# A decoder layer on one core: the rows of a block turned one block later, next to the turn-in, and three smaller moves

## The chip, the core and the metric

The kernel runs on one core of a Trainium2 chip. The metric is the device time of one execution in microseconds; "before" is the median of three runs. All data are fp32. The engines are TensorE (PE), VectorE (DVE), ScalarE (ACT), GpSimd (POOL) and SyncE (SP), which here issues nearly all DMA.

## What is computed

There are 16 x 256 = 4096 tokens of 256 channels, and three sublayers, each followed by a layer norm. Cut to what matters:

```python
# 1: squared-relu attention against fixed keys and values, 4 heads of 64 channels
q = layernorm(x, ln_g, ln_b).reshape(B, T, 4, 64)      # k = w_fc rows, v = w_proj.T rows: 1024 x 64
out = square(relu(einsum(q, k))) @ v
x = layernorm(x + (x + out))                            # so 2 x + out is normalized
# 2: cross attention, 16 heads of 16 channels, to ctx (16 batches of 256 rows)
attn = gamma * (Q K^T) / 4 + delta * (alpha_pos * max(D, 0) + alpha_neg * min(D, 0))   # D = clip(frac_k - frac_q, +-0.2)
x = layernorm(x + softmax(attn) V Wo^T + bo)
# 3: feed-forward of 1024 with the low-rank term of one expert of eight, chosen by argmax of the gate
x = layernorm(x + relu(x Wi^T + b + lora[top1](x)) Wo^T + b2)
```

## The kernel before

Everything is written in an order of its own (`tc.manual_schedule()`, L941): each engine runs its instructions in the order in which the program emits them, and waits come from the data and from tile pools, whose buffers are reused in turn. A pool's tile with `bufs=2` makes the third request wait until all readers of the first are done. So the order of emission is the order of each queue, SP's and GpSimd's too.

**Stage one** (L965 to L1044) is the first sublayer, in eight blocks of 512 rows (class Block, L249). A block is kept as `x` (four tiles of 128 rows), and is normalized, turned (128x128 transposes on TensorE) into `xnT` (channels on partitions, two halves `c`), and then goes through 16 pairs (c, n): `scores` (L327), four 64x64 matmuls into a tile of two PSUM banks (pool psA, two such tiles, four banks), a relu on ScalarE (L340), a square on VectorE (L342); and `values` (L345), four 64x64 matmuls that add into two banks of psV. The loop over m (L1022) takes eight steps a block: two scores, the values of the step before (`behind`), and then the pieces that the lists `steps[m]` hold. After the last values of a half c, `keep` (L360) copies the sums to `oT`, with two ScalarE copies and a GpSimd addition (L367); for c = 0 that is in step 4, for c = 1 in step 0 of the next block. In the steps of block tb lie, beside that:

- step 0: the last two rows of `norm_out` for block tb - 2 (L987)
- step 1: `turn_out` of block tb - 1 (L369): eight transposes of `oT` in two one-bank tiles of psB, each read by a VectorE instruction that makes y = 2 x + out (L383); then `measure_out(0)`, row statistics on VectorE (L185, L186); step 2: `measure_out(1)`
- steps 3 and 4: `measure` of the next block, and in step 3 the load of x of the block after that
- step 5: `scale` (L962): Ln and Exp on ScalarE (L194, L196) and four small VectorE instructions (L202 to L240), for eight rows of statistics: four of the next block's input, four of the last block's output
- step 6: `norm_in` of the next block, four ScalarE rows (L245)
- step 7: between the scores and the values, `turn_in` of the next block, eight transposes (L313), one half read by ScalarE (L317) and one by VectorE (L322); after the values two rows of `norm_out` of block tb - 1: a ScalarE instruction (L245) and a GpSimd addition of `bo` (L407) for each tile of 128 rows

Blocks 2 to 6 also make the clipped differences of `frac` that stage two needs (`clip`, L538: one VectorE instruction, L528, and for some batches a DMA to DRAM) in steps 0 and 7 (`slots`, L955). Block 1 also computes `biases` (L139), block 7 also the first batch's turn, keys and queries for stage two (`early`, L958; L1018 to L1021), with the queries in step 6, read by ScalarE (L481).

**Stage two** (L1059 to L1203) runs 64 groups (16 batches of four groups; a group is four heads of 256 x 256 logits) with the logits, maxima, exponentials and `attend` of neighbouring groups interleaved. psA's four banks become the four banks of logits. The feed-forward of a block of 512 rows (second class Block, L748) is spread over eight groups, part 0 to 7, from n = 15 on. In part 1, `gates` (L800) multiplies by the gate and the low-rank weights (128x64 matmuls) and copies the result on ScalarE (L813); it stands after the large piece of that group, `queries` (L461), and before `turned(2)`, `turned(3)` (L675, transposes) and their exponentials (L690). The large piece has two halves, TensorE's and the read of its bank (L476 on VectorE in these groups). `late` (L1154) says whether the second half is emitted at once or only after those exponentials. Banks for transposes and these products come from `tile_b` (L50): psB's two, and every third request psV's "W".

Of the kernel before, what the change touches and what calls it, by code (L numbers as in the profile page):

```python
# [14 lines left out]
P = 128  # L15
# [7 lines left out]
def tile_decoder_layer(ctx: ExitStack, tc: tile.TileContext, a: dict, out: bass.AP):  # L23
# [208 lines left out]
    if True:  # L232
# [16 lines left out]
        class Block:  # L249
# [119 lines left out]
            def turn_out(self, jj):  # L369
# [4 lines left out]
                ps = tile_b()  # L374
# [15 lines left out]
                )  # L390

# [353 lines left out]
    if True:  # L745
        out_view = out.rearrange("(b j p) c -> b p j c", j=4, p=P)

        class Block:  # L748
# [51 lines left out]
            def gates(self):  # L800

                ps = tile_b()
                for c in range(CC):
                    for t in range(2):
                        nc.tensor.matmul(
                            ps[64 * t : 64 * t + 64, 0:256],
                            lhsT=gw[:, c, :],
                            rhs=self.xT[:, c, 256 * t : 256 * t + 256],
                            start=(c == 0),
                            stop=(c == CC - 1),  # L810
                        )
                self.gT = small.tile([P, 256], FP, tag="spread", bufs=1, name="gT")
                nc.scalar.copy(self.gT, ps[:, 0:256])  # L813
# [127 lines left out]
    with tc.manual_schedule():  # L941
# [13 lines left out]
        slots = [(tb, m) for tb in range(2, 7) for m in (0, 7)]  # L955
        assert len(slots) == len(clips)
        first = batches[0]
        early = [first.turned(), first.keys(), first.queries(), first.vals()]  # L958
# [6 lines left out]
        for tb in range(NB):  # L965
# [4 lines left out]
            if tb == 0:  # L970
                nc.vector.memset(mv, 0.0)
            if 0 < tb < NB - 1:
                last = rows_in[tb - 1]
                for jj in range(2):
                    steps[1].append(lambda jj=jj: [*last.turn_out(jj)])
                steps[1].append(lambda: last.measure_out(0))
                steps[2].append(lambda: last.measure_out(1))
                last.mv = mv[:, 4:8]
                for j in range(2, 4):
                    steps[7].append(  # L980
                        lambda j=j, tb=tb: last.norm_out(by[tb], 4 + j, j, nc.gpsimd)
                    )
            if tb > 1:
                older = rows_in[tb - 2]
                for j in range(2):
                    steps[0].append(
                        lambda j=j, tb=tb: older.norm_out(by[tb - 1], 4 + j, j, nc.gpsimd)  # L987
                    )
            if tb + 1 < NB:
                nxt = rows_in[tb + 1]  # L990
                steps[3].append(lambda: nxt.measure(0))
                steps[4].append(lambda: nxt.measure(1))
                steps[5].append(lambda tb=tb, mv=mv: scale(tb, mv))
                steps[6].append(lambda tb=tb: nxt.norm_in(by[tb]))
                nxt.mv = mv[:, 0:4]
                turning = [lambda: nxt.turn_in(0), lambda: nxt.turn_in(1)]
            else:
                turning = []
            if tb + 2 < NB:
                steps[3].append(rows_in[tb + 2].load)  # L1000
# [17 lines left out]
            if tb + 1 == NB:  # L1018
                steps[4] += [lambda: groups[0].negative(3)]
                for m, together in ((4, early[:2]), (6, early[2:3])):  # L1020
                    steps[m] += [lambda p=piece: step(p) for piece in together * 2]  # L1021
            for m in range(8):  # L1022
# [4 lines left out]
                if m == 7:  # L1027
                    for piece in turning:
                        piece()
# [5 lines left out]
                for piece in steps[m]:  # L1035
                    piece()
        for block, *args in behind:
# [21 lines left out]
        for n in range(N + 2):  # L1059
# [22 lines left out]
            if n == N:  # L1082
                six.gates()
            if n > N:
                six.inner(0, range(0, 1))
            if older and not halved and not apart and n != N:
                if 0 <= n - 1 - FIRST < 8 * FUSED and (n - 1 - FIRST) % 8 in (5, 7):
                    groups[n - 3].attend()
                older.attend()
            if nxt:  # L1090
# [36 lines left out]
            else:  # L1127
                if nxt:
                    nxt.positive(0)
                    nxt.positive(1)  # L1130
                if last:
# [22 lines left out]
            late = (n % 4 == 0 or n == 1) and not ff  # L1154
# [9 lines left out]
            if ff and part == 1 and n < N:  # L1164
                ff.gates()
# [63 lines left out]
        seven.gates()  # L1229
        seven.inner(0, range(0, 1))  # L1230
# [85 lines left out]
```

## Time and profile before

| what | value |
|---|---|
| median of three runs | 903.74 us (903.57 to 930.24) |
| the profiled execution | 903.41 us, span 901.6 us, clock 0.999 |
| stage one, first scores to last values | 9.4 to 255.1 us |
| stage two with the fused feed-forward | 255.1 to about 824 us |
| last feed-forward blocks | to 901.6 us |
| PE busy in 9.44 to 255.10 | 245.08 of 245.66 us |
| PE busy in 345 to 824 | 478.05 of 479.00 us |
| DVE, ACT, POOL busy in 9.44 to 255.10 | 207.14, 178.52, 55.62 us |
| L342 squares, 128x1024 | 128 of them, mean 1255 ns |
| L340 relus, 128x1024 | 128 of them, mean 1022 ns |

How to read the profile lines: in a timeline, the columns are start (us), time from the first start to the last end (us), engine, line of the kernel, operation, output <- inputs, tile sizes and count; neighbouring instructions of one line are merged into one row, and in brackets stands how long the engine sat idle before it and for what. An fp32 matmul shows as two records. In the list of waits, the columns are total us, number, and longest us.

### The profile page before, as it was taken

How to read it: one execution, taken by the hardware profiler on the slowest of the kernel's cores; microseconds unless marked ns; L12 is line 12 of the kernel's file. 1: busy time of each engine (PE TensorE's matmuls, PEld its weight loads, DVE VectorE, ACT ScalarE, POOL GpSimd, SP SyncE). 2: the span in 40 equal slices, each digit the busy share in tenths (PEclk: the TensorE clock that was granted, in tenths of full speed). 3: DMA queues.
4: the chain of work that ended last, by engine and by line, in shares of the span. 5: the costliest groups of instructions: out<-in, count | busy, mean ns of one | idle time of the engine just before them, and what ended most of it. 6: DMA issues, size and time to landing. Idle time of an engine off the chain costs nothing.

```text
span 901.6 us, 19050 instructions
## 1 busy us (share of the span) xinstructions
PE 888.9 (99%) x6940; PEld 546.7 (61%) x6940; DVE 710.4 (79%) x1976; ACT 569.2 (63%) x947; POOL 394.7 (44%) x385
## 2 busy tenths in 40 slices
PE   8999999999999999999999999999999999999997
PEld 4333333333366777577668757766875786586555
DVE  6888899889669999778777887877788787778444
ACT  5767787778687888366565846656684675566111
POOL 1102312231569998435633654563465357344010
PEclk9999999999999999999999999999999999999999
DMA  5411011100001222010111102011110201111101
GB/s 139 147 36 36 31 39 39 65 2 1 13 1 54 70 70 57 13 42 21 36 48 39 48 14 66 20 36 46 41 49 13 67 18 38 42 28 44 23 1 47
DMA packets 44190, 37.01 MB, mean 41 GB/s; under 512 B 14912, under 2 KB 40000, under 8 KB 44096
## 3 DMA queue, kind: packets, MB, share of 16 engines
q1 hardware_dynamic: 43520, 35.52, 14.5%
q8 instruction: 55, 0.90, 0.4%
q14 instruction: 39, 0.32, 0.1%
q10 hardware_dynamic: 576, 0.26, 0.1%
HBM read 21.07 MB, written 6.03 MB: 30 GB/s over the span
## 4 chain that ended last, share of the span: by engine, by line
PE 83%; DVE 10%; ACT 4%; issue 2%; DMA 1%; SPq 1%; DVEq 0%; ACTq 0%
PE ps_l L876 12%; PE ps_b L683 11%; PE ps_v L352 10%; PE ps_a L332 10%; PE ps_b L906 7%; PE ps_l L643 6%; PE ps_v L699 6%; PE ps_v L906 4%; PE ps_b L595 3%; PE ps_b L465 3%; DVE pr L342 3%; PE ps_b L491 2%; PE ps_b L513 2%; DVE neg L658 2%; PE ps_l L888 2%
## 5 line engine op out<-in xcount | busy, mean ns | idle before, releaser
L622 POOL TENSOR_SCALAR neg<-dneg,aneg,delta 128x512 f32<-128x512 f32 x217 | 189.0, 882 | 183.5 <-PE ps_b L683 125.3
L658 DVE CUSTOM_DVE_ANT_0 neg<-ps_l,neg 128x256 f32<-128x256 f32 x512 | 181.4, 420 | 26.5 <-PE ps_l L643 23.6
L634 ACT ACTIVATE ps_l<-dpos,apos_d 128x512 f32<-128x512 f32 x256 | 173.2, 687 | 41.4 <-DVE mx L658 36.8
L342 DVE TENSOR_TENSOR pr<-r 128x1024 f32<-128x1024 f32 x128 | 155.4, 1255 | 33.5 <-ACT r L340 33.3
L690 ACT ACTIVATE pT<-ps_b 128x512 f32<-128x512 f32 x256 | 142.6, 590 | 56.3 <-PE ps_b L683 54.3
L340 ACT ACTIVATE r<-ps_a 128x1024 f32<-128x1024 f32 x128 | 126.4, 1022 | 57.3 <-PE ps_a L332 32.8
L683 PE MATMUL ps_b<-ident,neg 128*128 128x128 f32 x1024 | 138.8, 277 | 2.1 <-ACT pT L690 2.0
L683 PEld LDWEIGHTS ps_b<-ident,neg 128*128 128x128 f32 x1024 | 113.2, 141 | 37.4 <-issue 16.1
L673 POOL TENSOR_TENSOR neg<-neg,mx 128x1024 f32<-128x1024 f32 x65 | 124.2, 1912 | 22.8 <-DVE mx L658 21.7
L352 PE MATMUL ps_v<-pr,vv 64*64 64x512 f32 x1024 | 123.4, 593 | 0.3
L332 PE MATMUL ps_a<-xnT,kT 64*64 64x512 f32 x1024 | 122.1, 592 | 0.5 <-ACT r L340 0.3
L876 PE MATMUL ps_l<-xt,wi 128*128 128x512 f32 x248 | 111.5, 595 | 0.0
L673 DVE TENSOR_TENSOR neg<-neg,mx 128x1024 f32<-128x1024 f32 x63 | 95.7, 1519 | 0.3
L367 POOL TENSOR_TENSOR xt<-xt,half 128x512 f32<-128x512 f32 x15 | 23.8, 1584 | 136.9 <-ACT half L366 136.9
L352 PEld LDWEIGHTS ps_v<-pr,vv 64*64 64x64 f32 x1024 | 38.1, 132 | 70.6 <-issue 44.3
L332 PEld LDWEIGHTS ps_a<-xnT,kT 64*64 64x64 f32 x1024 | 37.8, 133 | 67.6 <-issue 54.8
L876 PEld LDWEIGHTS ps_l<-xt,wi 128*128 128x128 f32 x248 | 45.3, 190 | 49.0 <-issue 44.4
L643 PE MATMUL ps_l<-kM,qT 32*128 32x256 f32 x1024 | 74.1, 400 | 0.0
L407 POOL TENSOR_TENSOR hid<-hid,bo 128x256 f32<-128x256 f32 x32 | 29.4, 935 | 89.6 <-ACT hid L245 70.8
L906 PE MATMUL ps_b<-wof,hT 128*128 128x256 f32 x304 | 68.4, 380 | 0.0
L699 PE MATMUL ps_v<-pT,vaug 128*32 128x256 f32 x1024 | 66.4, 384 | 0.0
L899 DVE TENSOR_SCALAR hT<-ps_l,wib 128x512 f32<-128x512 f32 x43 | 29.8, 745 | 43.8 <-PE ps_l L888 43.8
(129 smaller groups left out, 1082.6 us busy)
## 6 DMA issues: line engine op xcount, KB each, us to landing
cT<-in_ctxT SPq DMA_DIRECT2D x16, 256.0 KB
kM<-keys SPq DMA_DIRECT2D x128, 32.0 KB
v<-raw SPq DMA_DIRECT2D x128, 32.0 KB
invs<-rows SPq DMA_DIRECT2D x128, 32.0 KB
x<-in_x SPq DMA_DIRECT2D x7, 512.0 KB
out<-x SPq DMA_DIRECT2D x7, 512.0 KB
frow<-in_frac SPq DMA_DIRECT2D x16, 128.0 KB
wi<-in_wiT SPq DMA_DIRECT2D x1, 1024.0 KB
```

The costliest lines, as they stand in the source:

```text
L332: nc.tensor.matmul(sc[64 * k : 64 * k + 64, h, :], lhsT=kT[64 * h : 64 * h + 64, q, hf * P + 64 * k : hf * P + 64 * k + 64], rhs=self.xnT[ ...
L342: nc.vector.tensor_tensor(pr, r, r, ALU.mult)
L352: nc.tensor.matmul(self.acc[k][64 * h : 64 * h + 64, :], lhsT=vv[64 * k : 64 * k + 64, hf, 64 * q : 64 * q + 64], rhs=pr[64 * k : 64 * k + ...
L622: nc.gpsimd.tensor_scalar(self.neg[:, g], self.batch.dneg, aneg[:, h : h + 1], delta, ALU.mult, ALU.mult,)
L634: nc.scalar.activation(banks[g], self.batch.dpos.rearrange("p j k -> p (j k)"), AF.Copy, scale=apos_d[:, h : h + 1],)
L643: nc.tensor.matmul(banks[g][:, j * S : (j + 1) * S], lhsT=self.batch.qT[rows, self.o, j * P : (j + 1) * P], rhs=self.batch.kM[rows, self.i ...
L658: nc.vector.tensor_tensor_reduce(out=self.t[:, g, j, :], in0=banks[g][:, j * S : (j + 1) * S], in1=self.neg[:, g, j, :], scale=1.0, scalar ...
L673: eng.tensor_tensor(rows, rows, top.to_broadcast([P, 4, S]), ALU.subtract)
L683: nc.tensor.transpose(ps[:, k * S + j * P : k * S + (j + 1) * P], self.t[:, g, j, k * P : (k + 1) * P], ident,)
L690: nc.scalar.activation(self.pT[:, g, :], self.ps[g], AF.Exp)
L876: nc.tensor.matmul(self.banks[g], lhsT=wi[:, c, f * P : (f + 1) * P], rhs=self.xT[:, c, :], start=(c == 0), stop=False,)
L906: nc.tensor.matmul(ps[:, 0:C], lhsT=self.hT[f][:, j * P : (j + 1) * P], rhs=wof[:, f, :], start=(f == 0), stop=(f == FC - 1),)
```

## The change

- Rows out: `turn_out` of block tb - 1 moves from step 1 of block tb to after its last step, as `turn_rows`, eight transposes into one two-bank tile of psA (the pool of the scores) in place of two tiles of psB. Its two L383 instructions follow there.
- `turn_in` of the next block moves from step 7's middle to right behind `turn_rows`, so that nothing stands between it and the next block's scores.
- `measure_out` of block tb - 2 is in steps 1 and 2, its four rows of `norm_out` in step 6 (three) and step 7 (one); `scale` is in step 4, after `measure(1)`; `norm_in` in step 5; the clips in steps 5 and 6; the load of x of block tb + 1 in step 0 of block tb.
- The first batch's queries move from step 6 to step 7 of block 7, and VectorE reads them.
- Stage two: `gates` stands after `attend`, before `turned(0)`, with its copy (`keep_gates`) after `positive(1)`; the second half of `queries` in these groups is late.

```diff
@@ -366,12 +366,13 @@
                 nc.scalar.copy(half, self.acc[1])
                 nc.gpsimd.tensor_tensor(self.oT[:, c, :], self.oT[:, c, :], half, ALU.add)

-            def turn_out(self, jj):
+            def turn_out(self, jj, ps=None):
                 if self.tb >= NB - 2:
                     self.y = hid[:, 4 * self.tb : 4 * self.tb + 4, :]
                 elif jj == 0:
                     self.y = px.tile([P, 4, C], FP, tag="y", bufs=1, name="y")
-                ps = tile_b()
+                if ps is None:
+                    ps = tile_b()
                 for j in range(2):
                     for c in range(CC):
                         nc.tensor.transpose(
@@ -388,6 +389,12 @@
                     ALU.mult,
                     ALU.add,
                 )
+
+            def turn_rows(self):
+
+                ps = psA.tile([P, 2, 512], FP, tag="A", name="ps_a")
+                for jj in range(2):
+                    [*self.turn_out(jj, ps[:, jj, :])]

             def turn_both(self):
                 first, second = self.turn_out(0), self.turn_out(1)
@@ -799,7 +806,7 @@

             def gates(self):

-                ps = tile_b()
+                ps = self.gps = tile_b()
                 for c in range(CC):
                     for t in range(2):
                         nc.tensor.matmul(
@@ -809,8 +816,10 @@
                             start=(c == 0),
                             stop=(c == CC - 1),
                         )
+
+            def keep_gates(self):
                 self.gT = small.tile([P, 256], FP, tag="spread", bufs=1, name="gT")
-                nc.scalar.copy(self.gT, ps[:, 0:256])
+                nc.scalar.copy(self.gT, self.gps[:, 0:256])

             def route(self):
                 ps = tile_b()
@@ -952,10 +961,10 @@
         clips = [
             (batches[b], which) for b in [*range(2, MADE), 0, 1] for which in ("dneg", "dpos")
         ]
-        slots = [(tb, m) for tb in range(2, 7) for m in (0, 7)]
+        slots = [(tb, m) for tb in range(2, 7) for m in (5, 6)]
         assert len(slots) == len(clips)
         first = batches[0]
-        early = [first.turned(), first.keys(), first.queries(), first.vals()]
+        early = [first.turned(), first.keys(), first.queries(True), first.vals()]
         behind = []
         by = [None] * (NB + 1)

@@ -967,37 +976,32 @@
             steps = [[] for _ in range(8)]

             mv = small.tile([P, 8, 2], FP, tag="mv8", bufs=2, name="mv8")
-            if tb == 0:
+            if tb in (0, 1, NB - 1):
                 nc.vector.memset(mv, 0.0)
-            if 0 < tb < NB - 1:
-                last = rows_in[tb - 1]
+
+            if tb > 1:
+                last = rows_in[tb - 2]
+                last.mv = mv[:, 4:8]
                 for jj in range(2):
-                    steps[1].append(lambda jj=jj: [*last.turn_out(jj)])
-                steps[1].append(lambda: last.measure_out(0))
-                steps[2].append(lambda: last.measure_out(1))
-                last.mv = mv[:, 4:8]
-                for j in range(2, 4):
-                    steps[7].append(
+                    steps[1 + jj].append(lambda jj=jj: last.measure_out(jj))
+                for j in range(4):
+                    steps[6 + j // 3].append(
                         lambda j=j, tb=tb: last.norm_out(by[tb], 4 + j, j, nc.gpsimd)
                     )
-            if tb > 1:
-                older = rows_in[tb - 2]
-                for j in range(2):
-                    steps[0].append(
-                        lambda j=j, tb=tb: older.norm_out(by[tb - 1], 4 + j, j, nc.gpsimd)
-                    )
+            turning = []
             if tb + 1 < NB:
                 nxt = rows_in[tb + 1]
-                steps[3].append(lambda: nxt.measure(0))
-                steps[4].append(lambda: nxt.measure(1))
-                steps[5].append(lambda tb=tb, mv=mv: scale(tb, mv))
-                steps[6].append(lambda tb=tb: nxt.norm_in(by[tb]))
                 nxt.mv = mv[:, 0:4]
-                turning = [lambda: nxt.turn_in(0), lambda: nxt.turn_in(1)]
-            else:
-                turning = []
-            if tb + 2 < NB:
-                steps[3].append(rows_in[tb + 2].load)
+                if tb:
+                    steps[0].append(nxt.load)
+                for jj in range(2):
+                    steps[3 + jj].append(lambda jj=jj: nxt.measure(jj))
+                steps[5].append(lambda tb=tb: nxt.norm_in(by[tb]))
+                if tb:
+                    turning.append(rows_in[tb - 1].turn_rows)
+                turning += [lambda: nxt.turn_in(0), lambda: nxt.turn_in(1)]
+            if tb + 1 < NB or tb > 1:
+                steps[4].append(lambda tb=tb, mv=mv: scale(tb, mv))
             if tb == 0:
                 steps[0] += [load_cross]
                 steps[2] += [load_ffn]
@@ -1017,16 +1021,13 @@
                 steps[5].append(batches[1].load)
             if tb + 1 == NB:
                 steps[4] += [lambda: groups[0].negative(3)]
-                for m, together in ((4, early[:2]), (6, early[2:3])):
+                for m, together in ((4, early[:2]), (7, early[2:3])):
                     steps[m] += [lambda p=piece: step(p) for piece in together * 2]
             for m in range(8):
                 c, n2 = divmod(m, 4)
                 coming = []
                 for n in (2 * n2, 2 * n2 + 1):
                     coming.append((now, c, n, now.scores(c, n)))
-                if m == 7:
-                    for piece in turning:
-                        piece()
                 for block, c, n, pr in behind:
                     block.values(c, n, pr)
                     if n == 7:
@@ -1034,6 +1035,8 @@
                 behind = coming
                 for piece in steps[m]:
                     piece()
+            for piece in turning:
+                piece()
         for block, *args in behind:
             block.values(*args)
         scored.close()
@@ -1081,12 +1084,15 @@
                 now.logits()
             if n == N:
                 six.gates()
+                six.keep_gates()
             if n > N:
                 six.inner(0, range(0, 1))
             if older and not halved and not apart and n != N:
                 if 0 <= n - 1 - FIRST < 8 * FUSED and (n - 1 - FIRST) % 8 in (5, 7):
                     groups[n - 3].attend()
                 older.attend()
+            if ff and part == 1 and n < N:
+                ff.gates()
             if nxt:
                 nxt.negative(4 if 1 <= n < FIRST - 1 or (ff and part < 2) else 3)
             if prep:
@@ -1128,6 +1134,8 @@
                 if nxt:
                     nxt.positive(0)
                     nxt.positive(1)
+                if ff and part == 1 and n < N:
+                    ff.keep_gates()
                 if last:
                     last.turned(0)
                     last.exps(0)
@@ -1151,7 +1159,7 @@
             if inverse:
                 inverse.invert()
             step(large_piece)
-            late = (n % 4 == 0 or n == 1) and not ff
+            late = n == 1 or n % 4 == 0 and (not ff or part == 1)
             if not late:
                 step(large_piece)

@@ -1161,8 +1169,6 @@
                 ff.turn(nc.scalar.copy)
                 if nxt:
                     nxt.positive(3)
-            if ff and part == 1 and n < N:
-                ff.gates()
             divided = batches[b - 2] if og == 0 and b >= 2 else None
             if divided and ff:
                 divided.divide()
@@ -1227,6 +1233,7 @@
         seven.biased()
         six.finish(2)
         seven.gates()
+        seven.keep_gates()
         seven.inner(0, range(0, 1))
         seven.route()
         seven.inner(0, range(1, 3))
```

## The prediction, made before the changed kernel was run

> **What bounds the kernel.** I read the page's busy shares and its chain first, then the timeline of TensorE through stage one, then ScalarE, VectorE and GpSimd over one block of it.
>
> ```profile
> PE 888.9 (99%) x6940; PEld 546.7 (61%) x6940; DVE 710.4 (79%) x1976; ACT 569.2 (63%) x947; POOL 394.7 (44%) x385
> ...
> PEclk9999999999999999999999999999999999999999
> ...
> PE 83%; DVE 10%; ACT 4%; issue 2%; DMA 1%; SPq 1%; DVEq 0%; ACTq 0%
> ```
>
> TensorE is the bound at full clock, so time comes or goes only where its stream gets shorter or gets a hole. "99%" doesn't show holes, because a matmul that waits can be drawn longer; the start-to-start distance does. TensorE, block 5 (its steps 3, 4 and 7, the turn, and the first scores of block 6):
>
> ```profile
> 173.52 2.22 PE L352 MATMUL ps_v<-pr,vv 64*64 64x512 f32 x16
> 175.57 1.90 PE L332 MATMUL ps_a<-xnT,kT 64*64 64x512 f32 x16
> ...
> 185.87 1.90 PE L332 MATMUL ps_a<-xnT,kT 64*64 64x512 f32 x16
> 187.69 1.09 PE L313 MATMUL ps_b<-ident,xn 128*128 128x128 f32 x8
> 188.72 1.95 PE L352 MATMUL ps_v<-pr,vv 64*64 64x512 f32 x16
> 190.48 1.90 PE L332 MATMUL ps_a<-xnT,kT 64*64 64x512 f32 x16
> ```
>
> Undisturbed, eight score or value matmuls (16 records) take 1.72 us to the next start, so a step of both takes 3.43 and eight steps 27.47. A turn of eight transposes costs 1.18: 185.87 to 190.48 is 4.61 against 3.43. Step 3 has a hole of 0.33 (173.52 to 175.57 is 2.05, not 1.72): squares of VectorE are late. A full block is 27.47 + 2 x 1.18 + 0.33 = 30.16; blocks 2 to 6 start 30.2 apart. ScalarE in block 5:
>
> ```profile
> 180.21 2.16 ACT L340 ACTIVATE r<-ps_a 128x1024 f32<-128x1024 f32 x2
> 182.37 0.30 ACT L194 ACTIVATE ln<-mv,epst 128x8 f32<-128x8 f32 x1
> 182.71 0.21 ACT L196 ACTIVATE near<-ln 128x8 f32<-128x8 f32 x1
> 183.57 2.16 ACT L340 ACTIVATE r<-ps_a 128x1024 f32<-128x1024 f32 x2 [0.66 <-PE ps_a L332]
> 185.63 2.06 ACT L245 ACTIVATE xn<-x,nm,rs 128x256 f32<-128x256 f32 x4
> ```
>
> The Ln stands behind the relus of step 5. A relu gives back the bank that the scores of the next step want; whatever is put ahead of it on ScalarE delays TensorE once the slack is used up. VectorE and GpSimd, blocks 4 to 5:
>
> ```profile
> 161.44 1.19 DVE L528 CUSTOM_DVE_ANT_1 dpos<-frow,nfcol 128x512 f32<-128x512 f32 x1
> ...
> 166.99 3.09 DVE L342 TENSOR_TENSOR pr<-r 128x1024 f32<-128x1024 f32 x2 [1.49 <-ACT r L340]
> ```
>
> ```profile
> 160.55 1.53 POOL L407 TENSOR_TENSOR hid<-hid,bo 128x256 f32<-128x256 f32 x2 [8.34 <-ACT hid L245]
> ...
> 166.60 2.40 POOL L407 TENSOR_TENSOR hid<-hid,bo 128x256 f32<-128x256 f32 x2
> ```
>
> Two squares take 2.36 undisturbed and 3.09 beside two additions of GpSimd; a clip of 0.66 takes 1.19.
>
> **The change, part by part: blocks 2 to 6.** I write times from the start of step 5's scores, with durations from these rows: relus 0.91 apart (1.91 for two, the second visible 1.0 long), rows of 128x256 on ScalarE 0.49 apart (2.06 for four), squares 1.13 apart, statistics of two tiles 1.1, TensorE to ScalarE 0.25, ScalarE or VectorE to TensorE 0.1.
>
> (1) *Ln and Exp a step earlier.* scale() moves from step 5 to step 4, behind measure(1) of the same step. VectorE's squares of step 4 start 2.15 into it and take 2.25, the statistics follow: they are ready at 2.13 of step 5. ScalarE now does Ln and Exp before the relus of step 5, so it stands until 2.16; Ln, Exp, then relu a 2.71 to 3.70 and b 3.62 to 4.62 (undisturbed a starts at 1.1). The scores of step 6 are due at 3.43 and get their first bank at 3.80, the second at 4.72 instead of 4.66: a hole of **0.43**. Before, measure(1) had a whole step of cover (Ln at 182.37 right after relus that had to be done anyway).
>
> (2) *norm_in in step 5.* Four rows, 4.52 to 6.48, stand ahead of the relus of step 6 as before they stood ahead of those of step 7, but on a late ScalarE: relu a 6.48 to 7.48, so step 7's scores, due at 7.30, start at 7.58, their second half at 8.49 instead of 8.44: **0.33**. ScalarE then does three norm_outs (to 9.76), the relus of step 7 (10.76, 11.67) and the last norm_out (12.06). Values of step 6 end at T = 11.07.
>
> (3) *The turns together.* Now eight transposes of turn_rows, then eight of turn_in, and no values between turn_in and the scores that need it. The first bank is free (10.76 + 0.1 < T). The first half of turn_in is issued at T + 0.11 + 12 x 0.117 = T + 1.51; 0.25 to ScalarE, 0.775 for its L317 row, 0.1 back: scores at T + **2.64**, against 2 x 1.18 = 2.36 for two separate turns: **+0.28**. Without that wait the sixteen would take 0.11 + 1.87 + 0.1 = 2.1. The Trainium skill (TensorEngine Tiling (Array Packing), Key Properties) says that changing the tiling mode drains TensorE; the rows price one visit from 64x64 to 128x128 and back at 1.18 - 8 x 0.117 = 0.24. By the rule alone this part would gain 0.24 a block; the wait for xnT eats it.
>
> (4) *The bank of turn_rows.* The second scores of the next block take its bank and wait for both L383 additions (0.6 + 0.67) on VectorE, behind the squares and step 6's clip. GpSimd's additions of three norm_outs (0.73 each, from 8.9) now fall beside those. The Trainium skill (SBUF — State Buffer, Who interferes with whom) says that a VectorE instruction with two SBUF inputs and a GpSimd one that reads SBUF exclude each other for the whole instruction. Undelayed, L383 ends at 14.37, and the bank is there at 14.47; it is wanted at T + 2.64 + 0.86 = 14.57: cost 0. By the rule, an addition getting in ahead of clip and both squares, it ends at 16.1: 1.6. By the row, 3.09 - 2.36 = 0.73 for two additions, 1.1 for three: 15.57 - 14.57 = **1.0**, which I take.
>
> (5) *What goes away.* L383 no longer lies in step 1, so VectorE keeps pace (3.33 for squares and statistics in a step of 3.43) and the hole of step 3 closes: **-0.33**.
>
> Per block 0.43 + 0.33 + 0.28 + 1.0 - 0.33 = 1.71, times five = **+8.6**.
>
> **The other blocks.** Block 0: holes 0.47 and 0.33 by the same reckoning, no norm_outs; its one turn gets 0.11 + 4 x 0.117 + 1.125 = 1.70 instead of 1.18: **+1.3**. Block 1: the transposes and matmuls of biases() lie ahead of the scores of steps 5 and 6 and cover Ln; turn +0.28, a small hole gone: **+0.2**. Block 7: the norm_outs of its start go away and with them a hole of 0.2; it measures rows there, on VectorE with 1 us to spare a step: **-0.2**. Its Ln needs statistics long done; three norm_outs before the relus of step 7 end 0.1 before these are due.
>
> **Moves that I cost at nothing.** The load of x (SP) goes out at a block's start once L383 has read the old rows, about 2.4 in; 512 KB were in about 4.5 us after the issue at 46.6, and measure(0) reads it some 14 in. Clips with their frow loads and writes, 0.33 to 0.42 of SP each, find SP idle. Two memsets of 0.07 find VectorE idle. In block 7 the four additions of GpSimd, 2.9, pass the second group's L622, which were done at 249.3 with nothing to do until 258.1. The first queries go past the last scores: the same matmuls, read by VectorE (2 x 0.54) at 5.6 to 6.7 of step 7; TensorE needs them at 3 x 1.72 + 1.93 = 7.1. Each us past that is a us, once.
>
> **Stage two.** In six groups gates() goes ahead of turned(). Queries then are followed by transposes (1.73 from L491 to L906) and not by gates (1.82): -0.09 each; attend to gates isn't in the trace, -0.1 to +0.1. Its copy (372 ns) goes ahead of exps(0): done at 356.34 where queries would take that bank at 356.5; 0.1 of cover. L476 no longer holds up VectorE (0.80 idle), but the maxima behind it wait for logits anyway. I take **-0.3** in all, ends -1.1 and +0.7.
>
> **Sum.** 8.6 + 1.3 + 0.2 - 0.2 - 0.3 = +9.6. The profiled execution took 903.41 (span 901.6, 1.8 around it), 0.3 below the median 903.74. So 913.0, 1.0% over the median.
>
> **Rivals.**
> A, *no exclusion* (ports don't collide, L383 is in time): part (4) costs 0, 5 less: 908. For it: clip and additions may interleave kindly; against it the 3.09.
> B, *not slower*: TensorE never reaches the waits. For it speaks the list of waits:
>
> ```profile
> PEld ps_a L332 <- ACT r L340: 4.7, 10, 1.2
> ```
>
> Scores hardly ever waited for a relu. Then only turns count: at 2.64 a block gives 0.28 - 0.33, five times -0.05, with block 0 at +0.5, block 1 at +0.2, -0.2 and -0.3: 903.4; with the xnT wait hidden too (2.1), 899 to 900. It decides if the statistics of step 4 are ready 0.4 earlier. Against it: the order on ScalarE leaves nothing else to do meanwhile.
> C, *x too late*: the load waits for L383, then measure, Ln and norm_in wait for it. From 12 us to landing each us is one a block; 15 us would give six times 3, 18 more: 931. Against it the 4.5 us.
>
> **Chances.** My sum 0.55 (own range 909 to 917), A 0.20, B 0.18, C 0.03, heavier collisions (rule's end of part 4, 916, and more) 0.04. The likeliest is 913.0. Leaving out most of B below 903.5 (0.13) and what lies above 918 (0.06) gives 903.5 to 918. Two per cent, about what a measurement of this kernel tells from no change, is 18 us: faster 0.01, same 0.94, slower 0.05.
>
> **What would show it.** Right: relus of step 5 start about 2.7 after its scores with Ln before them and idle ScalarE ahead of Ln; L332 of steps 6 and 7 0.4 and 0.3 late; scores 2.6 after the last values of step 6; the second scores of a block later by L383; steps 1 to 4 in 3.43; stage two as long as before. Wrong: blocks 2 to 6 30.2 apart or less, or time that goes in stage two, where I see no hole to close.

## The result, and the profile after

The changed kernel takes 929.19 us (median of six runs, 927.21 to 936.47) against 903.79 before (six runs): a ratio of 1.0298, with an interval of 1.0272 to 1.0323. The ratio compares means of fast runs, without the one of before at 930.24, which was in a slower state. The forecast was 913.0 within 903.5 to 918, so the direction was right and the size was not. The profiled execution took 929.1 (span 927.3), 25.7 more than that of before.

The page of the changed kernel, busy shares and chain:

```profile
PE 893.4 (96%) x6940; PEld 548.6 (59%) x6940; DVE 721.7 (78%) x1984; ACT 566.4 (61%) x947; POOL 397.5 (43%) x385
...
PE 70%; DVE 18%; ACT 7%; issue 3%; SPq 1%; DMA 1%; POOL 0%; DVEq 0%; ACTq 0%; POOLq 0%
```

TensorE has the same 6940 matmul records in nearly the same busy time (893.4 against 888.9), but VectorE's share of the chain grew from 10% to 18%: TensorE now waits for VectorE somewhere. The timeline of TensorE in block 5 (its steps 6 and 7, the turn, the first scores of block 6) says where; the last column is the idle time ahead of an instruction and what ended it:

```profile
198.08 2.01 PE L332 MATMUL ps_a<-xnT,kT 64*64 64x512 f32 x16
...
201.86 2.00 PE L332 MATMUL ps_a<-xnT,kT 64*64 64x512 f32 x16
203.68 1.90 PE L352 MATMUL ps_v<-pr,vv 64*64 64x512 f32 x16
205.51 0.66 PE L378 MATMUL ps_a<-ident,xt 128*128 128x128 f32 x4
209.32 0.65 PE L378 MATMUL ps_a<-ident,xt 128*128 128x128 f32 x4 [3.16 <-DVE y L384]
209.81 1.04 PE L313 MATMUL ps_b<-ident,xn 128*128 128x128 f32 x8
211.28 1.95 PE L332 MATMUL ps_a<-xnT,kT 64*64 64x512 f32 x16 [0.43 <-ACT xnT L317]
```

Four transposes of the old rows, then 3.16 us of nothing, then the other four. The fifth waits for the first addition (L384, L383 before). In the code: turn_rows uses up turn_out(0) to its end, addition included, before turn_out(1) issues its transposes. Both write one tile, so the second half's write is held until the read of the first half is over, although it goes to another bank of it. VectorE and GpSimd at that place:

```profile
205.26 3.41 DVE L342 TENSOR_TENSOR pr<-r 128x1024 f32<-128x1024 f32 x2
208.59 0.67 DVE L384 SCALAR_TENSOR_TENSOR y<-x,ps_a 128x512 f32<-128x512 f32 x1
```

```profile
203.28 5.97 POOL L414 TENSOR_TENSOR hid<-hid,bo 128x256 f32<-128x256 f32 x4 [6.29 <-ACT hid L245]
```

The addition stands behind the squares of step 7, which take 3.41 instead of 2.36 beside four additions of GpSimd. This happens at five boundaries in full (3.15 to 3.2 us) and at a sixth, where no such additions run, for 0.97. In the list of waits:

```profile
PE ps_a L378 <- DVE y L384: 16.8, 6, 3.2
```

Something else follows from the idle time. Windows of 3.4 us around the ends of blocks 2, 3 and 4 (start and end; busy time of PE, PEld, DVE, ACT, POOL; then TensorE's granted clock, DMA share, GB/s):

```profile
101.93:105.33 3.40, 0.59 (x5) 0.59 (x6) 2.76 (x3) 0.00 (x0) 2.74 (x2) 1.00 0.11 42
105.34:108.74 3.40, 3.38 (x17) 1.85 (x19) 1.50 (x2) 0.78 (x1) 0.00 (x0) 0.50 0.22 71
108.76:112.16 3.40, 3.40 (x36) 1.15 (x32) 2.07 (x2) 2.49 (x4) 0.00 (x0) 1.00 0.36 124
136.06:139.46 3.40, 0.88 (x8) 0.42 (x4) 3.40 (x4) 1.21 (x2) 3.40 (x3) 1.00 0.21 80
139.48:142.88 3.40, 2.78 (x12) 2.42 (x12) 1.25 (x2) 0.78 (x1) 0.55 (x1) 0.50 0.02 5
142.89:146.29 3.40, 3.38 (x33) 1.28 (x36) 1.95 (x2) 1.94 (x2) 0.00 (x0) 1.00 0.63 195
170.20:173.60 3.40, 1.78 (x16) 0.60 (x12) 3.40 (x3) 2.12 (x3) 3.40 (x4) 1.00 0.21 77
173.61:177.01 3.40, 1.53 (x12) 1.29 (x12) 2.46 (x4) 0.73 (x1) 1.47 (x1) 1.00 0.02 5
```

At the ends of blocks 2 and 3 the clock falls to 0.50 for one stretch of 3.4 us and then is full again; at the ends of blocks 4, 5 and 6 it doesn't fall. The two falls begin 34.13 us apart (105.34 and 139.47), ten times 3.413, but 3.8 and 2.5 us after the idle stretches began. (In e2_steps_back, below, five falls lie 37.55, 37.54, 34.14 and 37.54 apart: 11, 11, 10 and 11 times 3.413.) So they lie on a grid, and the windows above are laid on it. The clock fell after a window in which TensorE was busy for only 0.59 or 0.88 us. At the end of block 4 the idle stretch is as long, but it lies across two windows, with 1.78 and 1.53 busy, and the clock stayed. The runs differ in how often it falls: that of 927.21 had a mean clock of 0.999, that of 936.47 one of 0.985. The page's row of clocks, in tenths of 23 us slices, shows only nines.

### The profile page after: what moved, and what is told of

It reads as the page before. It is cut to its first block, busy times and chain, and to the rows that moved or that the text cites. A ratio compares the mean times of both kernels' runs of the same rounds, so it can differ in the third digit from the quotient of the medians.

```text
span 927.3 us, 19073 instructions
## 1 busy us (share of the span) xinstructions
PE 893.4 (96%) x6940; PEld 548.6 (59%) x6940; DVE 721.7 (78%) x1984; ACT 566.4 (61%) x947; POOL 397.5 (43%) x385
## 4 chain that ended last, share of the span: by engine, by line
PE 70%; DVE 18%; ACT 7%; issue 3%; SPq 1%; DMA 1%; POOL 0%; DVEq 0%; ACTq 0%; POOLq 0%
PE ps_l L885 12%; PE ps_b L690 11%; DVE pr L342 9%; PE ps_b L915 7%; PE ps_l L650 6%; PE ps_v L706 6%; PE ps_a L332 5%; PE ps_v L352 4%; PE ps_v L915 4%; PE ps_b L602 3%; ACT r L340 3%; PE ps_b L472 2%; PE ps_b L498 2%; DVE st L185 2%; PE ps_b L520 2%
## 5 line engine op out<-in xcount | busy, mean ns | idle before, releaser
L629 POOL TENSOR_SCALAR neg<-dneg,aneg,delta 128x512 f32<-128x512 f32 x217 | 184.2, 863 | 182.3 <-PE ps_b L690 127.6
L342 DVE TENSOR_TENSOR pr<-r 128x1024 f32<-128x1024 f32 x128 | 158.2, 1277 | 37.9 <-ACT r L340 37.0
L340 ACT ACTIVATE r<-ps_a 128x1024 f32<-128x1024 f32 x128 | 124.1, 1021 | 51.4 <-PE ps_a L332 45.8
L332 PE MATMUL ps_a<-xnT,kT 64*64 64x512 f32 x1024 | 124.2, 600 | 3.9 <-ACT xnT L317 2.2
L352 PE MATMUL ps_v<-pr,vv 64*64 64x512 f32 x1024 | 121.4, 589 | 0.0
L367 POOL TENSOR_TENSOR xt<-xt,half 128x512 f32<-128x512 f32 x15 | 19.1, 1274 | 180.5 <-ACT half L366 180.5
L332 PEld LDWEIGHTS ps_a<-xnT,kT 64*64 64x64 f32 x1024 | 35.5, 133 | 78.2 <-issue 48.5
L414 POOL TENSOR_TENSOR hid<-hid,bo 128x256 f32<-128x256 f32 x32 | 41.2, 1310 | 73.3 <-ACT hid L245 54.5
```

The source lines that it names most:

```text
L332: nc.tensor.matmul(sc[64 * k : 64 * k + 64, h, :], lhsT=kT[64 * h : 64 * h + 64, q, hf * P + 64 * k : hf * P + 64 * k + 64], rhs=self.xnT[ ...
L340: nc.scalar.activation(r, sc, AF.Relu)
L342: nc.vector.tensor_tensor(pr, r, r, ALU.mult)
L352: nc.tensor.matmul(self.acc[k][64 * h : 64 * h + 64, :], lhsT=vv[64 * k : 64 * k + 64, hf, 64 * q : 64 * q + 64], rhs=pr[64 * k : 64 * k + ...
L629: nc.gpsimd.tensor_scalar(self.neg[:, g], self.batch.dneg, aneg[:, h : h + 1], delta, ALU.mult, ALU.mult,)
```

## The experiments

Ratios are to the kernel before, with their intervals. Line numbers are those of each kernel.

### e1_both_halves: the transposes ahead of the additions

```
-                for jj in range(2):
-                    [*self.turn_out(jj, ps[:, jj, :])]
+                both = [self.turn_out(jj, ps[:, jj, :]) for jj in range(2)]
+                for half in both * 2:
+                    next(half, None)
```

> The changed kernel, but the eight transposes of turn_rows are issued ahead of both additions of the old rows, instead of four, an addition, four, an addition. Theory (the order of issue within one bank pair is the cause: the fifth transpose waits for an addition that reads the other half, and that addition stands behind the squares of step 7): the 3.2 us of idle TensorE at each of five boundaries go; the wait moves to the second scores, where my forecast had it, at about 1.0; a block from 34.2 to about 31.9, TensorE's clock 0.999 again, in all 913 (910 to 917). First rival (rows in a bank of the scores cost this wherever the addition stands; the wait only moves to the second scores in full): 922 or more. Second rival (VectorE is too busy at the boundary, or the clock fell for another reason): 925 or more, clock still 0.985 to 0.995.

Measured: 915.26, ratio 1.0129 [1.0116, 1.0143], four runs within 0.5, clock 0.998 to 1.000. The timeline of TensorE at the end of block 5:

```profile
195.91 1.09 PE L378 MATMUL ps_a<-ident,xt 128*128 128x128 f32 x8
196.84 1.04 PE L313 MATMUL ps_b<-ident,xn 128*128 128x128 f32 x8
198.31 1.09 PE L332 MATMUL ps_a<-xnT,kT 64*64 64x512 f32 x8 [0.43 <-ACT xnT L317]
200.43 1.09 PE L332 MATMUL ps_a<-xnT,kT 64*64 64x512 f32 x8 [1.03 <-DVE y L384]
```

Eight transposes in a row; the next block's scores come 2.50 after the last values (those end at T, 0.1 ahead of 195.91; the forecast said 2.64), and the second scores wait 1.03 for L384 (the forecast said 1.0). A block is 32.06. Three moved lines are worth 13.9 of the 25.4 us, and both rivals fall. This is the kernel that the forecast had priced; what it leaves over is taken up below.

### e9_two_tiles: the order kept, each half in a tile of its own

```
-                ps = psA.tile([P, 2, 512], FP, tag="A", name="ps_a")
                 for jj in range(2):
+                    ps = psA.tile([P, 2, 512], FP, tag="A", name="ps_a")
                     [*self.turn_out(jj, ps[:, jj, :])]
```

> The changed kernel with its order of issue (four transposes, addition, four transposes, addition), but each half in a tile of its own, so in both bank pairs of the scores. Theory (the wait of 3.2 is one of the fifth transpose for an addition that reads the other half of the same tile; it is made where the program's parts of one tile are told apart no finer): the eight transposes follow each other without a stop; both first scores of the next block then wait for the additions, 1.4 for the first and no more for the second: a block of about 32.4 against 32.06 in e1_both_halves and 34.2, 917 (915 to 919), clock 0.999. Rival (TensorE can't write a bank beside an addition that VectorE has pending, whatever the tile): 925 or more with TensorE idle ahead of the second four transposes.

Measured: 916.25, ratio 1.0142 [1.0129, 1.0156], as expected. The timeline of TensorE at the end of block 5:

```profile
196.56 1.21 PE L378 MATMUL ps_a<-ident,xt 128*128 128x128 f32 x8
...
200.49 1.95 PE L332 MATMUL ps_a<-xnT,kT 64*64 64x512 f32 x16 [1.84 <-DVE y L384]
```

With the order of the changed kernel, but two tiles, the eight transposes run without a stop (the first starts at 196.56, the next row at 197.61), and the next scores wait 1.84 instead. So an addition that is still pending doesn't stop TensorE; sharing one tile does. Order and tile are both needed for the loss, and mending either gains 13 to 14 of the 25.4 us.

### e4_filled_wait: the wait kept, TensorE kept busy in it

```
+                idle = tile_b()
                 for jj in range(2):
+                    if jj:
+                        for j in range(20):
+                            nc.tensor.transpose(
+                                idle[:, j % 4 * P : (j % 4 + 1) * P], ident, ident
+                            )
                     [*self.turn_out(jj, ps[:, jj, :])]
```

> The changed kernel with extra work: twenty transposes of the identity into a bank nobody reads, between the two halves of turn_rows, where TensorE stood idle for 3.2 us. Theory (the lower clock of 0.985 to 0.995 and the spread of 927 to 936 come from these idle stretches alone): the wait for the addition stays, so a block stays at 34.2 where the clock was full, but the clock is 0.999 in every run and the times lie together at 925 to 927. Rival (the clock falls for another reason): the spread of some 9 us stays and clocks under 0.995 are seen. Rival (TensorE's twenty transposes last longer than the wait): time above 930 at a clock of 0.999.

Measured: 927.94 (927.74 to 928.25), ratio 1.0270 [1.0256, 1.0284]. TensorE at the end of block 5:

```profile
205.30 2.35 PE L400 MATMUL ps_b<-ident 128*128 128x128 f32 x20
208.63 0.66 PE L378 MATMUL ps_a<-ident,xt 128*128 128x128 f32 x4 [0.98 <-DVE y L384]
```

The twenty transposes took 2.35 of the wait and 0.98 was left idle; clocks are 0.999 to 1.000 in all five runs, where the changed kernel had 0.985 to 0.999. So the idle stretches cost the clock and spread the runs over 9 us; the wait itself costs what the fastest run of the changed kernel shows (927.21). The time is 0.9 over the expected 925 to 927; in block 1, whose wait of 0.97 is shorter than twenty transposes, the edit adds 1.0. The Trainium skill (TensorE: Matmul & The Clock Gate, Part 1: The HAM clock gate) says that TensorE falls to half clock after about 3.4 us of idleness, in a window that runs free of the kernel. The trace agrees with the half clock (0.50), with the length (3.41) and with a grid that doesn't follow the blocks. It differs in one point: the window need not be idle throughout; 2.8 and 2.5 idle of 3.4 were enough (0.59 and 0.88 busy). The rule did not stand in the forecast, since no idle time of that length did.

### e2_steps_back: what it measured instead

To e1_both_halves: Ln and Exp back in step 5, norm_in in step 6, two norm_outs in step 7, and two in step 0 of the next block, all as before.

```
+            if tb > 2:
+                older = rows_in[tb - 3]
+                for j in range(2, 4):
+                    steps[0].append(
+                        lambda j=j, tb=tb: older.norm_out(by[tb - 1], 4 + j, j, nc.gpsimd)
+                    )
```

> As e1_both_halves, and Ln and Exp go back to step 5, norm_in to step 6, two of the four norm_outs to step 0 of the next block. Theory (steps 1 and 2 of the forecast are worth 0.43 and 0.33 a block in blocks 2 to 6 and about 0.8 in block 0): 4.6 below e1_both_halves, about 908. Rival (they are hidden as soon as the scores start late, so putting them back gives nothing): within 1 of e1_both_halves. Rival (norm_outs at the block's start and norm_in ahead of the relus of step 7 delay the addition of the old rows further): above e1_both_halves.

Measured: 937.21, ratio 1.0378 [1.0363, 1.0392]; clock 0.987 to 0.992. All three expectations missed the size; the last had the sign. VectorE in block 5, whose first scores start at 173.87:

```profile
181.06 1.28 DVE L384 SCALAR_TENSOR_TENSOR y<-x,ps_a 128x512 f32<-128x512 f32 x2 [8.27 <-ACT hid L245]
```

y is a tile with one buffer. The next rows can be added into it only when all four norm_outs have read the old ones; two of them now came a block later, and VectorE stood idle for 8.27 us ahead of its addition. This edit can't tell what steps 1 and 2 of the forecast are worth. It shows what turn_rows at the block's end asks for: all four norm_outs must be over by then. That does not need Ln and norm_in as early as the change puts them: e7_steps_back has both a step later, and all four norm_outs in time.

### e6_additions_later: GpSimd away from the squares

To e1_both_halves: norm_out leaves its addition of bo to step 4 of the next block.

```
-                eng.tensor_tensor(rows, rows, bo, ALU.add)
+                if eng:
+                    self.add_bias(j, eng)
...
+            if tb > 2:
+                older = rows_in[tb - 3]
+                for j in range(4):
+                    steps[4].append(lambda j=j: older.add_bias(j, nc.gpsimd))
```

> As e1_both_halves, but GpSimd's additions of bo to the rows turned out come in step 4 of the next block (behind the addition of half there) instead of beside the squares of step 7. Theory (part 4 of the forecast: these additions and VectorE's squares hold each other up, which makes two squares of step 7 take 3.4 instead of 2.36, and so the second scores of a block wait 1.0): two squares at 2.4, the wait of the second scores under 0.2, about 4 to 5 less than e1_both_halves: 910.5. Rival A (the additions don't matter, the old rows' additions come this late anyway): the wait stays at 0.8 to 1.0, 915. Rival (the same collision moves to steps 4 to 6 and costs there): within 1 of e1_both_halves, with longer squares in steps 5 and 6 and a hole behind them.

Measured: 913.26, ratio 1.0105 [1.0091, 1.0119]. Both the theory and its third rival have a part. The squares of step 7 take 2.36 again and the second scores wait for nothing, so rival A of the forecast (the additions don't matter) falls. But the collision moved. VectorE in steps 5 (first two rows) and 7 of block 5, and TensorE in its step 6:

```profile
186.24 0.55 DVE L202 SCALAR_TENSOR_TENSOR sd<-mv,near 128x8 f32<-128x8 f32 x1 [0.61 <-ACT near L196]
186.82 0.65 DVE L203 SCALAR_TENSOR_TENSOR sd<-sd,near 128x8 f32<-128x8 f32 x1
...
195.18 2.36 DVE L342 TENSOR_TENSOR pr<-r 128x1024 f32<-128x1024 f32 x2 [0.33 <-ACT r L340]
```

```profile
190.03 2.22 PE L352 MATMUL ps_v<-pr,vv 64*64 64x512 f32 x16 [0.85 <-DVE pr L342]
```

Operations on 8 columns, 0.17 each elsewhere, take 0.55 to 0.65 beside GpSimd's additions (0.70 each): the trace shows each of the four end just after one addition does. That is the exclusion for the whole instruction that the Trainium skill (SBUF — State Buffer, Who interferes with whom) states, and in proportion it strikes these short operations hardest: the four take 2.6 us (186.24 to 188.84) instead of 0.8. A block fell only from 32.06 to 31.82.

### e7_steps_back and e8_turn_between

To e6_additions_later, e7_steps_back: all four norm_outs in step 7, norm_in in step 6, scale in step 5. To that, e8_turn_between: the turn at the block's end in another order.

```
-                if tb:
-                    turning.append(rows_in[tb - 1].turn_rows)
                 turning += [lambda: nxt.turn_in(0), lambda: nxt.turn_in(1)]
+                if tb:
+                    turning.insert(1, rows_in[tb - 1].turn_rows)
```

> As e6_additions_later, and Ln and Exp back in step 5, norm_in in step 6, all four norm_outs in step 7. (e2_steps_back left two norm_outs in the next block, and the old rows' tile has one buffer, so the addition of the next rows waited for them.) Theory (steps 1 and 2 of the forecast, 0.43 + 0.33 a block as forecast, 0.35 + 0.36 as the trace of e1_both_halves has them, and 0.8 in block 0): 4.4 less than e6_additions_later, about 906. Rival (the four norm_outs in step 7 hold up xnT and the old rows' addition by as much): within 1 of e6_additions_later.

> As e7_steps_back, but the turn at the end of a block goes: first half of turn_in, turn_rows, second half of turn_in, so that the transposes of the old rows hide the wait for xnT. Theory (part 3 of the forecast: sixteen transposes with nothing to wait for take 2.1, against 2.5 with the wait for xnT): 0.4 a block in five or six blocks, 2 less than e7_steps_back, about 904. Rival (the second scores then wait for the old rows' additions, which come 0.5 later): within 0.5 of e7_steps_back.

Measured: 910.09, ratio 1.0070 [1.0056, 1.0083], and 909.92, ratio 1.0067 [1.0054, 1.0081]. Steps back: 3.2 gained, not 4.4. Block 2, in which no additions fall, went from 30.80 to 30.15 and block 0 from 28.74 to 28.00: 0.65 and 0.74 for steps 1 and 2. Blocks 3 to 6 gained only 0.3, as the collision of e6_additions_later holds up norm_in there; the other 0.6 lie in stage two. The other order gave nothing, as its rival said, but for another reason: xnT's row on ScalarE (L317) comes behind four norm_outs either way, and the first scores wait the same 0.76 for it; the second scores don't wait.

### Stage two: e3_stage_two_only, e5_queries_not_late, e10_gates_but_first

e3_stage_two_only is the kernel before with the stage-two lines of the change alone; e5_queries_not_late takes back one of them; e10_gates_but_first leaves the first group (n = 16) as before, with gates and their copy under the same condition.

```
e5:  -            late = n == 1 or n % 4 == 0 and (not ff or part == 1)
     +            late = (n % 4 == 0 or n == 1) and not ff
e10: -            late = n == 1 or n % 4 == 0 and (not ff or part == 1)
     +            late = n == 1 or n % 4 == 0 and (not ff or part == 1 and tb > 0)
```

> The kernel before, with only the stage-two part of the change: gates ahead of turned, their copy apart, later second half of the first queries in every group of four. Theory from the two traces (gates are worth about nothing in five groups of six; the copy of the late queries waits behind a division that waits for a transfer, and turned of the next block waits for it, once, in n = 16): +0.5 to +1.0, 904.3 to 904.8. Forecast's own figure: -0.3 (ends -1.1 and +0.7). Rival (all 1.5 us that stage two lost come from this part): 905.2.

> e3_stage_two_only without its later second half of the first queries in the feed-forward blocks (that line as before). Theory: the wait of 0.8 for the queries in n = 16 goes, and the 0.13 to 0.15 a group that the gates ahead of turned gave in e3_stage_two_only stays: about 0.8 less than e3_stage_two_only, 903.0. Rival (the wait in n = 16 comes from the gates' place or from their copy): no less than e3_stage_two_only, 903.8.

> e3_stage_two_only, but in the first feed-forward block (n = 16) gates and queries stand as before. Theory (in n = 16 alone the division that the queries now stand behind waits for a transfer, 0.85; in the five others the change gives 0.13 to 0.15 each): 0.9 less than e3_stage_two_only, 902.9, which is 0.8 under the kernel before. Rival (the gain of the five is only the loss of n = 16 being made up later): 903.7, like before.

Measured: e3 903.80, ratio 1.0002 [0.9994, 1.0010]; e5 907.01, 1.0038 [1.0024, 1.0052]; e10 902.70, 0.9990 [0.9982, 0.9999]. From the profile of e3, TensorE and VectorE in n = 16:

```profile
361.36 1.06 PE L683 MATMUL ps_b<-ident,neg 128*128 128x128 f32 x8 [0.82 <-DVE qT L476]
```

```profile
357.78 1.39 DVE L588 TENSOR_TENSOR oT<-v,invs 128x512 f32<-128x512 f32 x1 [0.96 <-DMA invs<-rows]
359.09 1.21 DVE L673 TENSOR_TENSOR neg<-neg,mx 128x1024 f32<-128x1024 f32 x1
360.23 0.99 DVE L476 TENSOR_SCALAR qT<-ps_b,qscale,bq_s 128x256 f32<-128x256 f32 x2
```

The late queries stand behind a division that waits for a transfer, and the next turned needs their bank: 0.85 lost, once. In each of the five later groups the change gains 0.12 to 0.15 (e3's delay falls from 1.06 to 0.36). e3 so ends near before's time, below the 904.3 to 904.8 that I had expected. e10 keeps the gain without the loss: 0.76 less than before at the end, as expected. My expectation of e5 was wrong by 4 us: with gates ahead of the queries these end 1.2 later in their group, and where VectorE still takes them in their old place it waits 1.81 for them instead of 0.80, about 0.5 a group. The late line is what makes the moved gates harmless.

### e11_combined and e12_rows_in_halves

e11_combined joins what had helped, with the additions of bo on VectorE in step 0 and the first half of turn_in ahead of the values of step 7; e12_rows_in_halves also splits y:

```
-                    self.y = px.tile([P, 4, C], FP, tag="y", bufs=1, name="y")
+                    self.y = [px.tile([P, 2, C], FP, tag=f"y{h}", bufs=1, name="y") for h in range(2)]
```

> What the runs so far favour, together: both halves' transposes ahead of the additions; Ln in step 5, norm_in in step 6, four norm_outs in step 7; the first half of turn_in between scores and values of step 7 (values hide the wait for xnT), turn_rows and the second half of turn_in at the block's end; the additions of bo on VectorE in step 0 of the next block, where it is idle; block 0 turned as before; stage two as in e10_gates_but_first. Theory: steps of 27.47 without a hole, 0.24 + 0.47 and 0.24 + 1.41 for two visits of the transposes, 29.83 a block against 30.18 before: five times 0.35, and 0.6 in block 7, 0.8 in stage two: 900.5 (899.5 to 902). Rival (the second scores wait for the old rows' additions, which wait for four norm_outs): 0.5 to 1.0 a block more, 903 to 906. Rival (additions on VectorE push squares and statistics of steps 1 to 4 late): 903 to 905, with holes in steps 1 to 4.

> As e11_combined, but the turned rows y of a block lie in two tiles of two rows each, so that the first addition of the next rows needs only the first two norm_outs done. Theory (in e11_combined the second scores wait 0.63 for the old rows' additions, which wait 1.2 for the last norm_out because y is one tile with one buffer): the wait goes, five times 0.63 or 3 less than e11_combined: 902.0, under the kernel before. Rival (the second addition alone, which still waits for the last norm_out, sets the time): half of it or less, 903.5 to 905.

Measured: e11 905.07, ratio 1.0018 [1.0011, 1.0025]: its first rival came true. TensorE at the start of block 6:

```profile
193.67 1.09 PE L332 MATMUL ps_a<-xnT,kT 64*64 64x512 f32 x8 [0.63 <-DVE y L384]
```

There L384 waits 1.18 for the last norm_out. With y in two tiles that wait is gone: e12 takes 902.55, ratio 0.9987 [0.9980, 0.9993], 2.5 less, and a block falls from 30.70 to 30.15. That is before's 30.18 and not the 29.83 that I had worked out. Of the 0.8 us between the profiles of before and e12, half lies in stage two, as in e10, and half in stage one, there mostly in block 7. These two are the only versions faster than the kernel before, by 0.8 (e10) and 1.2 us (e12).

## Why the prediction failed

A block is counted from its first scores to the next one's. In us against before, from the profiled executions:

| term | forecast | changed kernel | e1_both_halves |
|---|---|---|---|
| (1) Ln a step earlier, per block | +0.43 | +0.43 | +0.46 |
| (2) norm_in in step 5 | +0.33 | +0.33 | +0.35 |
| (3) turns together | +0.28 | **+3.52** | +0.14 |
| (4) bank of turn_rows, second scores | +1.0 | +0.05 | +1.28 |
| (5) hole of step 3 | -0.33 | -0.33 | -0.33 |
| sum per block | 1.71 | 4.00 | 1.90 (a block: 1.88) |
| lower clock, all blocks | 0 | +2.1 | 0 |
| block 0 / block 1 | +1.3 / +0.2 | +1.2 / +1.4 | +1.2 / +0.2 |
| block 7 | -0.2 | -0.5 | (holds a wait of term 4) |
| stage two | -0.3 | +1.5 | +1.6 |

**Steps 1, 2 and 5 held** to the hundredth in the changed kernel: in its block 5 the scores of steps 6 and 7 start 0.32 + 0.11 and 0.23 + 0.10 late with Ln, four norm_ins and three norm_outs ahead of the relus, as forecast; steps 1 to 4 take 3.43 each.

**Step 3 failed.** It priced the turns at +0.28, and they cost +3.52. "Now eight transposes of turn_rows, then eight of turn_in" took sixteen transposes for an unbroken row. In fact TensorE stood for 3.16 us in the middle of it, ahead of the fifth transpose, and the scores came at T + 5.88 (211.28, with T at 205.40), not T + 2.64. This could be read from the diff: the loop in turn_rows consumes a generator whose last piece is an addition on another engine, and the second turn writes the tile that this addition reads. e1_both_halves and e9_two_tiles show that either of two edits, in order or in tile, removes the 3.2; of it 1.03 and 1.84 come back as waits of the next scores.

**Step 4 had the right cause at the wrong instruction.** The exclusion of GpSimd and VectorE, and an addition late by squares, were forecast and are there (3.41 for two squares; e6_additions_later takes the additions away and the wait goes). The same lateness costs 1.0 where the second scores wait, which are due 3.5 after T, and 3.2 where the fifth transpose waits, due 0.6 after T. In the changed kernel the second scores find the additions long done. In e1_both_halves the wait is where and as long as I had it; its 1.28 is 1.03 idle and 0.25 because the first eight matmuls don't overlap the next ones. The forecast put these waits in blocks 2 to 6; they fall in 3 to 7, five either way.

**The clock** was in no step. Five boundaries of over 3 us of idleness cost 2.1 us in the profiled execution (blocks 2 and 3 exceed the 4.00 by 0.4 and 1.7), and the slowest run lies 9 over the fastest.

**Block 1** gets a turn_rows at its end too; the forecast counted only its 0.28 and not the wait (0.97 there).

**Stage two** was forecast at -0.3 with the claim "I see no hole to close"; alone (e3) it is worth 0.1, because a gain of 0.7 in five groups, near what was forecast for six, pays for 0.85 in n = 16. That late queries stand behind a division, and this behind a transfer, I had not followed: I asked what waits behind the queries, not what they would wait behind. In the changed kernel stage two is 1.1 longer than in e3, 0.5 of it by n = 15. That comes with the stage-one lines, and about half of it with the places of Ln, norm_in and the norm_outs: e7_steps_back, which differs from e6_additions_later in nothing else, has a stage two 0.6 shorter (647.84 against 648.44). In e11 nothing of it is left (646.36, against 646.28 in e10). How those places reach into stage two stays open.

**The rivals.** A (no exclusion) is refuted by e6_additions_later, B (not slower) and C (x too late) by the first trace: the only statistics that wait for x are those of block 0's own rows, at 3.52. None of them, and no case of mine, held a wait inside the turn itself, which comes, at 0.97, even at the boundary without such additions.

For e1_both_halves, the kernel that I had in fact priced, the sum of 9.6 stands against 12.0 in the profile and 11.6 in the medians: +9.0 in blocks 2 to 7, where 8.4 was forecast, and 1.9 more in stage two.

## What to carry to other kernels

When a helper that alternates between engines is called twice in a row, write out the order in which its pieces land on each queue, and ask of each piece which tile it shares with the one before: dependencies here went by the tile, not by the part of it that is touched, so one late reader stops the writer of the other half. Price a late operation at the first instruction that waits for it, in order of issue; the same delay was worth 1.0 at one waiter and 3.2 at another. A tile with a single buffer ties its last reader to its next writer, and moving either past the other costs a whole wait (8.27 us of VectorE in e2_steps_back).

## What the hardware showed that I had not expected

After idle stretches of 3.15 to 3.2 us TensorE ran, at some boundaries and not at others, at a granted clock of 0.50 for one window of 3.41 us. What decided in this trace was how the stretch lay on a grid of such windows: with 2.5 or 2.8 us of it in one window the clock fell, with it split over two it didn't. In e2_steps_back a stretch of 2.64 (106.42 to 109.06), all in the window from 106.29 to 109.70, was followed by 0.50 as well. Useless transposes in the gap (e4) kept it at 1.00. VectorE's operations on 128 x 8 elements took 0.65 instead of 0.17 beside GpSimd's additions: moved out of the way of long squares, these cost as much among four short operations.
